# Six ring buffers instead of five for streamed weights, ten resident weights instead of eleven

## The chip, the cores and the metric

The kernel runs on one core of a Trainium2 chip. TensorE (matmuls), VectorE (DVE), ScalarE (ACT) and GpSimd (POOL) work side by side, each through its own list of instructions in order; SyncE (SP) issues nearly all DMA transfers of this kernel, also in order. An instruction may wait for semaphores of other engines or of transfers, and whatever stands behind it on its engine waits with it. The metric is the time of one execution on the device in microseconds, the median of several runs.

## The reference

One layer of graph attention with a layer norm ahead of it, over 128 graphs of 128 nodes and 768 features, in float32:

```python
h = jnp.maximum(_layernorm(x, axis=-1), 0.0)
x = x + _L0_gnn_ref(h, adj, Wq, bq, Wk, bk, Wv, bv, beta)

# _L0_gnn_ref, with 12 heads of 64:
q = _split_heads(input_graph @ Wq + bq)        # k and v likewise
scores = jnp.einsum('bhqd,bhkd->bhqk', q, k) / jnp.sqrt(HD)
scores = scores + beta * adj_e
scores = jnp.where(adj_e > 0, scores, -9000000000000000.0)
probs = jax.nn.softmax(scores, axis=-1)
out = jnp.einsum('bhqk,bhkd->bhqd', probs, v)
```

## The kernel before

**Tiling.** Four graphs make a group: 512 rows of activations, and 32 groups in all (`G` from 0 to 31). Each group needs the product of its normalised, transposed activations with Wq, Wk and Wv. The weights are taken in three slices: `qk0` (the first half of the columns of q and k), `v`, and `qk1` (the second half of q and k).

**Products.** In groups 1 to 31 a slice is a 2x3 by 3x3 block product done with 15 block multiplications instead of 18 (the table `PRODUCTS`), and each of these with seven 128x128 zones instead of eight. A group is thus 3 x 15 = 45 products; this text calls their places in the order slots 0 to 44: 0 to 14 are qk0, 15 to 29 are v, 30 to 44 are qk1. "v.5" means row 5 of `PRODUCTS` in the slice v. Each product reads one combination of activations, which DVE has summed before, and one *prepared weight*: seven 128x128 float32 tiles, 448 KB. `product` (line 664) issues 28 matmuls at line 681.

**Prepared weights.** During group 0, which works with plain products (`plain_slice`, line 1029), DVE and POOL build all 45 prepared weights from the raw ones (`prepare`, line 367; sums at lines 380 to 386 and 403). Those whose place in `sequence` is named in `RESIDENT` stay in SBUF for good (tiles `res_qk`, `res_v`, line 360). The others are built in a buffer, stored to DRAM once (`kept`, line 389) and loaded anew in each of the groups 1 to 31. `home` (line 369) picks the buffer: while qk0 and v are prepared, three of eight non-resident weights are built in a buffer with tag "e" (which later hold the attention's exponentials), all others in the ring.

**The ring.** Streamed weights land in the `RING` buffers with tag "T". `ring` (line 431) lists them in the order of use. `load_T` (line 435) issues the next load on SP. It is called as many times as there are buffers during group 0 (twice within `prepare`, and for `n in range(2, RING)` at line 1319), and then once behind each streamed product, at line 685. SP's instruction waits until that product's matmuls have read their buffer; the weight that it fetches is the one used `RING` streamed products later. A product with a resident weight calls no load.

**Order.** From the slice v of group 0 on all instructions stand in an order written out by hand (`manual_schedule`, line 1284): `slice_z` (line 1009) emits product by product, and behind each one what the tables `TABLE`, `EVICT` and `DECODE` give for that time. The products' results leave PSUM through DVE (lines 704, 711) and ACT (lines 716, 724, 726), are decoded on POOL (lines 739 to 754), and go to scores (line 776), masking (line 789), the exponential (line 798) and attention (line 855). SP's list holds the loads of weights, the loads of x in two forms (lines 295 and 513), of adj (line 599), of the residual (`xo`, line 763) and the outputs (line 908).

Of the kernel before, what the change touches and what calls it, by code (L numbers as in the profile page):

```python
# [114 lines left out]
PORDER = (1, 0, 5, 2, 3, 10, 7, 6, 13, 11, 4, 9, 14, 8, 12)  # L115
XORDER = (1, 0, 5, 2, 3, 10, 6, 7, 13, 11, 4, 9, 14, 8, 12)
ORDER = {"qk0": (1, 0, 5, 2, 10, 3, 6, 7, 13, 11, 9, 4, 14, 12, 8), "v": (1, 0, 5, 2, 10, 3, 6, 7, 13, 11, 4, 9, 14, 8, 12), "qk1": (4, 1, 0, 8, 2, 5, 3, 6, 7, 10, 9, 13, 11, 12, 14)}
RING = 5
RESIDENT = (10, 12, 16, 17, 21, 29, 33, 36, 39, 41, 42)
EB = 3  # L120
HOMES = 8

# [104 lines left out]
def direct(ctx, tc, x, adj, wq, bq, wk, bk, wv, bv, beta, out, bad):  # L227
# [131 lines left out]
    sequence = [(sl, n) for sl in ("qk0", "v", "qk1") for n in ORDER[sl]]  # L359
    resident = {key: const.tile([P, 7, P], F32, name=f"res_{key[0]}_{key[1]}") for key in (sequence[at] for at in RESIDENT)}  # L360
    kept, tz = {}, {}
# [5 lines left out]
    def prepare(sl):  # L367

        def home(name):
# [4 lines left out]
            if sl != "qk1" and made_in[0] % 8 in (2, 5, 7):  # L374
                t = work.tile([P, 2, W], F32, tag="e", name=f"prep_{sl}_{n}", bufs=EB)
                return t.rearrange("p i w -> p (i w)")[:, 0:7 * P].rearrange("p (z n) -> p z n", n=P)
            return work.tile([P, 7, P], F32, tag="T", name=f"prep_{sl}_{n}", bufs=RING)

# [56 lines left out]
    def load_T():  # L435
        if nt[0] < len(ring):
            G, sl, n = ring[nt[0]]
            nt[0] += 1
            t = tz[G, sl, n] = work.tile([P, 7, P], F32, tag="T", name=f"T_{G}_{sl}_{n}", bufs=RING)
            nc.sync.dma_start(t, kept[sl, n])  # L440
# [751 lines left out]
    def then(at, f, *args):  # L1192
        todo.setdefault(at, []).append(lambda: f(*args))
# [6 lines left out]
    def bias(G, *at):  # L1200
        for n in at:
            then(n, bias_step, G)
# [115 lines left out]
    bias(1, 4, 6, 8)  # L1318
    for n in range(2, RING):
        then(10 + n, load_T)  # L1320
# [180 lines left out]
```

## Time and profile before

| | us |
|---|---|
| median of 3 runs | 2683.88 |
| lowest, highest | 2681.6, 2685.84 |
| the profiled execution's own time | 2675.62 |
| its span in the profile | 2673.7 |
| granted TensorE clock over the span | 0.998 of full |

The profile is of one execution. PE stands for the matmuls of TensorE and PEld for its weight loads, which overlap; SPq for SP as it issues DMAs. A group of instructions is written as line, engine, operation and tiles, out<-in, so `pair<-sbig,T_qk` at L681 are the matmuls of a product of qk0 or qk1 with a streamed weight, `res_qk` and `res_v` mark resident ones, and `T_v` streamed ones of the slice v. "Idle before <- X" says what ended an engine's idle time; "issue" means that the profile shows nothing that did. The ends of matmuls are modelled, so matmul rows of neighbouring products overlap a little, and starts are the better measure. In rows by stretch (us from the span's start) come the stretch's length, the busy time of PE, PEld, DVE, ACT and POOL with their number of instructions, the granted clock, the mean busy share of the 16 DMA engines and the GB/s that they moved; a share can come out a little over 1. In the chain of waits each row is a piece of the work that ended last: start, length, what.

### The profile page before, as it was taken

Reading aid. Unit: us, or ns where it says so; the run is one execution under the profiler, and the core shown is the slowest. Engines: PE = TensorE matmul, PEld = TensorE weight load, DVE = VectorE, ACT = ScalarE, POOL = GpSimd, SP = SyncE. Lnnn points to the kernel's source line nnn. Section 1 sums busy time; section 2 is a strip of 40 time slices with the busy share of each in tenths; the row PEclk is TensorE's granted clock in tenths of the full one; section 3 lists DMA queues with packets and bytes.
Section 4 is the critical chain, followed back from the end, with each engine's and each line's share of the span. In section 5 each row is a group of like instructions: output and inputs, shape, how many; then the busy total and the mean of one; then the engine's idle time right before and its main releaser. Section 6 shows DMA issues by size and latency. Waiting matters only on the chain.

```text
span 2673.7 us, 121363 instructions
## 1 busy us (share of the span) xinstructions
PE 2645.9 (99%) x52041; PEld 2565.2 (96%) x52041; DVE 2165.9 (81%) x2702; ACT 1754.7 (66%) x4608; POOL 2089.9 (78%) x3043
## 2 busy tenths in 40 slices
PE   9999999999999999999999999999999999999998
PEld 8799999999999999999999999999999999999997
DVE  7878887878887778888788877888887888778876
ACT  2567766677766677666777666776667776667654
POOL 4877778877778877788777788777887777887774
PEclk9999999999999999999999999999999999999999
DMA  8888888888888988888888888889888888888875
GB/s 247 270 272 270 276 280 272 275 287 262 285 279 272 282 269 271 281 278 269 280 265 283 278 272 267 274 271 285 272 272 280 265 282 280 265 277 275 249 247 165
DMA packets 526964, 721.97 MB, mean 270 GB/s; under 512 B 105932, under 2 KB 370648, under 8 KB 526424
## 3 DMA queue, kind: packets, MB, share of 16 engines
q1 hardware_dynamic: 525776, 713.38, 84.4%
q8 instruction: 411, 6.73, 1.0%
q14 instruction: 129, 1.06, 0.1%
q10 hardware_dynamic: 648, 0.79, 0.1%
HBM read 647.99 MB, written 66.05 MB: 267 GB/s over the span
## 4 chain that ended last, share of the span: by engine, by line
PE 95%; DMA 3%; DVE 1%; issue 0%; SPq 0%; ACT 0%; ACTq 0%; DVEq 0%
PE pair L681 78%; PE pair L776 7%; PE pair L855 6%; PE pair L1048 3%; DMA T_qk<-kept_qk 2%; DMA sbig<-in_L_gnn_Wk_dram 0%; PE pair L1265 0%; DVE home L704 0%; PE pair L1053 0%; DMA x<-in_x_dram 0%; SPq L336 0%; PE pair L926 0%; SPq L908 0%; DVE e L789 0%; DVE st L464 0%
## 5 line engine op out<-in xcount | busy, mean ns | idle before, releaser
L704 DVE TENSOR_TENSOR home<-home,pair 128x896 f32<-128x896 f32 x836 | 880.8, 1077 | 225.5 <-PE pair L681 192.7
L681 PE MATMUL pair<-sbig,T_qk 128*64 128x128 f32 x13020 | 833.0, 274 | 9.2 <-DMA T_qk<-kept_qk 6.9
L681 PEld LDWEIGHTS pair<-sbig,T_qk 128*64 128x64 f32 x13020 | 711.6, 137 | 28.7 <-issue 16.5
L739 POOL TENSOR_TENSOR home<-home 128x256 f32<-128x256 f32 x308 | 263.5, 855 | 339.3 <-DVE home L704 339.0
L681 PE MATMUL pair<-A,T_qk 128*64 128x128 f32 x6944 | 446.0, 273 | 0.3 <-issue 0.3
L855 PE MATMUL pair<-v,e 128*64 128x65 f32 x6048 | 412.6, 221 | 0.7 <-issue 0.7
L681 PE MATMUL pair<-T_v,sbig 128*64 128x128 f32 x6944 | 404.1, 273 | 2.1 <-issue 1.5
L681 PEld LDWEIGHTS pair<-T_v,sbig 128*64 128x64 f32 x6944 | 382.2, 137 | 8.3 <-ACT e L836 5.0
L836 ACT ACTIVATE e<-e,sm 128x64 f32<-128x64 f32 x1512 | 381.7, 341 | 5.0 <-DVE sm L824 3.4
L681 PEld LDWEIGHTS pair<-A,T_qk 128*64 128x64 f32 x6944 | 384.0, 137 | 0.4 <-issue 0.4
L855 PEld LDWEIGHTS pair<-v,e 128*64 128x64 f32 x6048 | 370.7, 137 | 3.8 <-issue 0.8
L724 ACT ACTIVATE home<-pair 128x640 f32<-128x640 f32 x340 | 240.4, 707 | 189.0 <-PE pair L681 187.7
L681 PE MATMUL pair<-sbig,res_qk 128*64 128x128 f32 x4340 | 314.0, 273 | 0.3
L742 POOL TENSOR_TENSOR home<-home 128x256 f32<-128x256 f32 x308 | 264.3, 858 | 24.1
L885 ACT ACTIVATE sm<-pair,tiny 128x8 f32<-128x8 f32 x189 | 50.8, 269 | 338.4 <-PE pair L855 338.4
L789 DVE SCALAR_TENSOR_TENSOR e<-pair,biasT 128x1024 f32<-128x1024 f32 x189 | 229.3, 1213 | 34.1 <-PE pair L776 33.1
L740 POOL TENSOR_TENSOR home<-home 128x256 f32<-128x256 f32 x308 | 230.6, 749 | 24.1
L681 PEld LDWEIGHTS pair<-sbig,res_qk 128*64 128x64 f32 x4340 | 240.5, 137 | 1.4 <-DVE home L704 1.3
L560 ACT ACTIVATE x<-x,block 128x192 f32<-128x192 f32 x480 | 222.6, 540 | 0.0
L726 ACT ACTIVATE home<-pair,bqk 128x128 f32<-128x128 f32 x680 | 214.1, 377 | 0.0
L798 ACT ACTIVATE e<-e 128x1024 f32<-128x1024 f32 x189 | 196.1, 1055 | 20.3 <-DVE e L789 12.7
L741 POOL TENSOR_TENSOR home<-home 128x128 f32<-128x128 f32 x308 | 180.4, 586 | 24.2
(208 smaller groups left out, 4489.9 us busy)
## 6 DMA issues: line engine op xcount, KB each, us to landing
T_qk<-kept_qk SPq DMA_DIRECT2D x713, 448.0 KB, 4.7
T_v<-kept_v SPq DMA_DIRECT2D x341, 448.0 KB, 4.7
xo<-in_x_dram SPq DMA_DIRECT2D x190, 256.0 KB, 5.3
out_dram<-xo SPq DMA_DIRECT2D x189, 256.0 KB, 5.2
x<-in_x_dram SPq DMA_DIRECT2D x248, 192.0 KB, 7.6
sbig<-in_x_dram SPq DMA_DIRECT2D x116, 384.0 KB
kept_qk<-prep_qk SPq DMA_DIRECT2D x23, 448.0 KB, 2.8
adj<-in_adj_dram SPq DMA_DIRECT2D x128, 64.0 KB, 4.1
```

The costliest lines, as they stand in the source:

```text
L560: nc.scalar.activation(t, t, AF.Relu, bias=shift[G, n], scale=rstd[G, n])
L681: nc.tensor.matmul(p[q:q + HD, at, :], lhs[:, q:q + HD], rhs, start=(first and at % 4 == 0), stop=True, skip_group_check=True)
L704: nc.vector.tensor_tensor(t, t, p[:, 0:7], op)
L724: nc.scalar.activation(t[:, 0:5], p[:, 0:5], AF.Copy, scale=float(sign))
L726: nc.scalar.activation(t[:, at], p[:, at], AF.Identity, bias=bqk[:, of, oc:oc + 1], scale=float(sign))
L739: e.tensor_tensor(t[:, 1:4:2], t[:, 1:4:2], twice(5), ALU.add)
L740: e.tensor_tensor(t[:, 2:5:2], t[:, 2:5:2], twice(1), ALU.add)
L742: e.tensor_tensor(t[:, 0:7:6], t[:, 0:7:6], twice(2), ALU.add)
L789: nc.vector.scalar_tensor_tensor(e[:, :, at], ps[:, :, at], SCORE_CAP * ISCALE, bias[:, :, at], op0=ALU.min, op1=ALU.add)
L798: nc.scalar.activation(e, e, AF.Exp, scale=1.0 / ISCALE)
L836: nc.scalar.activation(o[:, r, b, 0:HD], pa[:, r, b, 0:HD], AF.Copy, scale=t[:, 1, r, b:b + 1])
L855: nc.tensor.matmul(pa[q:q + HD, 2 * g + i, :], k[:, q:q + HD], vt[G, "v", r, h // 4][:, 4 * g + h % 4, :], start=True, stop=True, skip_gro ...
```

## The change

`RING` goes from 5 to 6, and place 17 leaves `RESIDENT`. Place 17 of `sequence` is the third product of the slice v, v.5: its prepared weight (the sum T6 of `SUMS_B`) is built in a buffer, stored once, and streamed in each of the 31 groups. A resident tile and a ring buffer have the same size, so SBUF use stays. The order of the products and all tables stay. The count of streamed weights in a group goes from 34 to 35.

```diff
--- before.py
+++ after.py
@@ -115,8 +115,8 @@
 PORDER = (1, 0, 5, 2, 3, 10, 7, 6, 13, 11, 4, 9, 14, 8, 12)
 XORDER = (1, 0, 5, 2, 3, 10, 6, 7, 13, 11, 4, 9, 14, 8, 12)
 ORDER = {"qk0": (1, 0, 5, 2, 10, 3, 6, 7, 13, 11, 9, 4, 14, 12, 8), "v": (1, 0, 5, 2, 10, 3, 6, 7, 13, 11, 4, 9, 14, 8, 12), "qk1": (4, 1, 0, 8, 2, 5, 3, 6, 7, 10, 9, 13, 11, 12, 14)}
-RING = 5
-RESIDENT = (10, 12, 16, 17, 21, 29, 33, 36, 39, 41, 42)
+RING = 6
+RESIDENT = (10, 12, 16, 21, 29, 33, 36, 39, 41, 42)
 EB = 3
 HOMES = 8
```

## The prediction, made before the result was known

> **What bounds the kernel now.** I read the page first, for the engine that sets the end.
>
> ```profile
> span 2673.7 us, 121363 instructions
> ...
> PE 2645.9 (99%) x52041; PEld 2565.2 (96%) x52041; DVE 2165.9 (81%) x2702; ACT 1754.7 (66%) x4608; POOL 2089.9 (78%) x3043
> ...
> PE 95%; DMA 3%; DVE 1%; issue 0%; SPq 0%; ACT 0%; ACTq 0%; DVEq 0%
> ```
>
> TensorE is busy 99% of the span, and the chain of waits is 95% TensorE: the matmul stream is the bound. The change removes no matmul. It can win only the time in which that stream stands still for a streamed weight, and the 3% of the chain that runs through DMA says where to look. Next is the chain of waits in order of time, a few starts from the whole run.
>
> ```profile
> 161.29 9.32 PE pair L681 x168
> ...
> 568.51 9.32 PE pair L681 x168
> ...
> 649.53 9.32 PE pair L681 x168
> ...
> 2525.49 9.32 PE pair L681 x168
> ```
>
> This run of 168 matmuls in 9.32 us stands at the same slot of each group. Two neighbours are 649.53 - 568.51 = 81.02 us apart: an undisturbed group. From 161.29 to 2525.49 there are 2364.2 us; 29 undisturbed groups make 29 x 81.02 = 2349.6. So all irregular waits of 29 groups together cost 14.6 us, a ceiling for the gain there. One such wait, in three views: the chain, the matmuls, and SP's DMA issues.
>
> ```profile
> 2543.48 6.02 DMA T_qk<-kept_qk
> ```
>
> ```profile
> 2543.47 1.70 PE L681 MATMUL pair<-res_v,A 128*64 128x128 f32 x28
> 2545.00 1.70 PE L681 MATMUL pair<-A,T_qk 128*64 128x128 f32 x28
> 2546.53 1.70 PE L681 MATMUL pair<-sbig,T_qk 128*64 128x128 f32 x28
> 2549.64 1.60 PE L681 MATMUL pair<-sbig,T_qk 128*64 128x128 f32 x25 [1.41 <-DMA T_qk<-kept_qk]
> ```
>
> ```profile
> 2540.36 1.63 SPq L440 DMA_DIRECT2D T_qk<-kept_qk  x1
> 2542.09 1.29 SPq L908 DMA_DIRECT2D out_dram<-xo  x1
> 2543.48 0.46 SPq L440 DMA_DIRECT2D T_qk<-kept_qk  x1
> ```
>
> An undelayed product takes 1.53 us (2545.00 - 2543.47 with a resident weight, 2546.53 - 2545.00 with a streamed one), so a streamed weight that is there in time costs TensorE nothing. The fourth product, slot 32 of its group (qk1.0), had its load issued at 2543.48; it took 6.02 us and came 1.41 us late. The load before it, for slot 31, went out at 2540.36. SP, which issues in order, lost the time between on that issue (1.63 us) and on an output (1.29).
>
> **How large the stall is.** The waits of TensorE on loads; the idles in front of weight loads that read T_qk, by what ended them; the same view of a group without a stall:
>
> ```profile
> PE pair L681 <- DMA T_qk<-kept_qk: 6.9, 9, 1.4
> ```
>
> ```profile
>   issue: 16.9, 73
>   DVE adj L613: 2.1, 2
> ...
>   DVE A L580: 1.4, 1
>   DVE biasT L617: 1.0, 1
>   DVE biasT L605: 0.7, 1
> ```
>
> ```profile
> PEld pair L681 <- issue: 0.5, 3, 0.2
> ```
>
> Lower bound: 6.9 us in 9 waits that the matmul side lays to the load. Upper bound, from the weight side: in qk the streamed weight is what is loaded into the array, so the wait stands there first, and the profile names "issue" or some DVE instruction for it. 16.9 + 2.1 + 1.4 + 1.0 + 0.7 = 22.1 us. A quiet group has three idles of 0.17 us at L681 (0.5 in all), two of them in front of T_qk, so 31 x 2 x 0.17 = 10.5 us are regular and 22.1 - 10.5 = 11.6 remain. I take 10.5, near the upper end, since the wait begins on the weight side and short ones show only there.
>
> **The change part by part.** *A sixth buffer.* SP issues at the same places of the program as before, but each issue fetches the weight that is used one streamed product later. So a load goes out, and lands, about when its predecessor did. In the stall above, slot 32's load takes the place at 2540.36 and is 2543.48 - 2540.36 = 3.1 us earlier, against 1.41 us of lateness: it is there in time. Where SP isn't behind, the shift is one product, 1.53 us, still over the longest wait of 1.4. It holds for slots 24 (v.11) to 44 and on through qk0. Gain 10.5 us, if transfers take as long as before.
>
> *v.5 streamed.* Product 5 of the slice v (slot 17) reads a resident weight now; it gets one load in each of 31 groups. Up to v.13 (slot 23) the sixth buffer is used up by v.5 itself, so the leads of v.2, v.10, v.3, v.7 and v.13 stay. What the new load meets: TensorE's weight loads, SP's issues, and the DMA share by stretch, all in one group, with the row of the loads and of all DMA from the page.
>
> ```profile
> DMA packets 526964, 721.97 MB, mean 270 GB/s; under 512 B 105932, under 2 KB 370648, under 8 KB 526424
> ```
>
> ```profile
> T_v<-kept_v SPq DMA_DIRECT2D x341, 448.0 KB, 4.7
> ```
>
> ```profile
> 1376.93 3.09 PEld L681 LDWEIGHTS pair<-res_v,sbig 128*64 128x64 f32 x56
> ```
>
> ```profile
> 1377.30 13.03 SPq L440 DMA_DIRECT2D T_v<-kept_v  x5
> ```
>
> ```profile
> 1380.10:1383.70 3.60, 3.60 (x98) 3.33 (x96) 1.65 (x2) 3.48 (x11) 3.32 (x5) 1.00 0.89 274
> 1383.70:1387.30 3.60, 3.60 (x72) 3.60 (x70) 3.27 (x5) 3.54 (x9) 3.33 (x6) 1.00 0.63 222
> 1387.30:1392.50 5.20, 5.20 (x112) 4.86 (x108) 3.97 (x6) 3.71 (x8) 4.15 (x8) 1.00 0.70 228
> 1406.00:1412.00 6.00, 6.00 (x128) 6.00 (x126) 4.66 (x6) 2.45 (x8) 5.69 (x9) 1.00 1.05 412
> ```
>
> 31 x 448 KB are 14.2 MB, 2.0% over the 721.97 MB of now. The 56 weight loads of res_v are the two resident products v.0 and v.5, which end near 1380.1. The new load goes out there. SP waits there for TensorE, and behind the new wait stand only other weight loads: from 1377.30 to 1390.33 SP issues nothing but L440, so no load of x, no output and no row is held up. From 1380.1 to 1392.5 the DMA engines have room: 0.11 x 3.6 + 0.37 x 3.6 + 0.30 x 5.2 = 3.3 us of all sixteen. One load is 458,752 bytes: 1.1 us at the 412 GB/s of the last row, 1.7 us at the mean of 270. That room hides it: 0 us. Without the room the loads behind it would land 1.1 to 1.7 us later, and where the shift is one product the gain would be gone.
>
> The Trainium skill's "DMA: Bandwidth & Descriptors", section Specifications, puts the limit of HBM for one core at about 358 GB/s. The trace does not agree: the stretch from 1406 moved 412 GB/s. By the page's figure the added bytes would be an estimated 14.2 MB / 358 GB/s = 40 us where nothing hides them; by the rows they fit into the idle share.
>
> *At the start.* The weight of v.5 is made by the same instructions and now also stored, once; which later weights of v are made in the ring and which in the buffers of e changes with it. The nearest rows:
>
> ```profile
> SPq L389 <- POOL prep_v L386: 14.0, 7, 3.7
> ```
>
> ```profile
> DVE prep_qk L403 <- POOL prep_v L386: 2.5, 1, 2.5
> ```
>
> SP waits for a weight to be ready for its store, 2.0 us on the mean, 3.7 at most; DVE waits 2.5 us once. One store more holds SP for up to 3.7 us, under plain products that keep TensorE going; a sixth buffer can save DVE its 2.5. Bounds on the path: -2.5 to +3.7 us. I take 0, since DVE at 81% and SP have time to spare and TensorE is the bound.
>
> *At the end* nothing is left to load: 0. Sum against the profiled execution: 2675.6 us (its span of 2673.7 and 1.9 around it) - 10.5 = 2665.1. That execution lies 8.3 us under the median of the timed runs, 2683.88; I carry the difference over: 2683.9 - 10.5 = 2673.4, or 0.39% faster. What is late next are the 0.17 us idles and a few single ones, which stay.
>
> **The rivals.** *Late loads stay late.* At the start of qk1 the DMA share is 1.05, so transfers queue; if the added load is not worked off by then, each landing there moves out by 1.1 to 1.7 us. For it: that share. Against it: the room of 3.3 us before, and a shift of 3.1 us where SP was behind. Gain 0 to 7, middle 3: 2681.
>
> *More was lost in the timed runs.* The 8.3 us between profile and median may be late loads too. For it: the stalls differ from group to group (none in the quiet one, 1.4 us in another), so they depend on more than the program. Against it: a constant part is as likely. Gain 10.5 + 8.3 = 18.8: 2665.
>
> *Instruction fetch*, the slower side. TensorE has idles that no semaphore ends:
>
> ```profile
> 2200.85 2.21 PEld L681 LDWEIGHTS pair<-T_v,sbig 128*64 128x64 f32 x40 [0.89 <-issue]
> ```
>
> ```profile
> q8 instruction: 411, 6.73, 1.0%
> ```
>
> This one lies in the first products behind the scores of v, where the new load will be in flight. I read it as a late fetch: 411 packets in 2673.7 us are one in 6.5 us, so each group has one near this place. If a fetch there waits until the new load has passed (middle 1.4 us) in all 31 groups, it costs 31 x 1.4 = 43 us; less 10.5 the time is 2683.9 + 33 = 2717. It decides from 8 groups on (8 x 1.4 = 11.2). For it: the place. Against it: loads are in flight nearly always already, and the ceiling for all irregular waits is 14.6 us.
> The Trainium skill's "DMA: Bandwidth & Descriptors", section Queues, rings and completion order, says that each DMA engine takes turns between queues packet by packet; by that rule a fetch waits for a packet and not for the load, the cost is near 0 and the time the forecast's. No run here shows the turns.
>
> **How the numbers follow.** Forecast 0.63, late loads 0.15, more to win 0.10, fetch 0.07, and 0.05 for a build that differs elsewhere, on the slow side. About 0.2% (5.4 us) is what a measurement of this kernel can tell from no change. Faster by more than that: forecast and second rival, 0.73. The same: most of the first rival, 0.14. Slower: fetch, the differing build and the rest, 0.13. The forecast's own range: 10.5 becomes 6.9 to 11.6 and the start -2.5 to +3.7, so 2670 to 2681. The whole range takes in the second rival's 2665 and the first rival's end at no gain, with 3.7 us at the start, each with some of the runs' scatter of 2 us: 2662 to 2688. Outside lies mostly the fetch.
>
> **What would show it.** Right: no wait of TensorE on T_qk above 0.3 us, groups 81.0 us apart nearly throughout, 341 + 31 = 372 loads of T_v, and 1% or less of DMA in the chain. Late loads: landings at the start of qk1 over 6 us and idles that remain there. Fetch: idles put down to "issue" behind the scores of v in most groups. The prediction is wrong if TensorE stops for DVE or ACT where it stopped for the load, with the same time per group, or if the groups stay as far apart as now.

## The result and the profile after

| | before | after |
|---|---|---|
| median, us (executions) | 2684.86 (4) | 2666.82 (4) |
| lowest to highest, us | 2681.6 to 2686.05 | 2664.59 to 2668.08 |
| the profiled execution's own time, us | 2675.62 | 2665.87 |
| its span, us | 2673.7 | 2664.1 |

The ratio of the times is 0.9934, with a 95% interval of 0.9917 to 0.9951: the change saves 18.0 us, or 0.66%. 2673.4 had been forecast, inside a range of 2662 to 2688 that holds the measured time. Measured between the two profiled executions the gain is only 9.75 us, near the 10.5 of the sum; the experiments had to explain the difference of the two gains as well as the gain.

From the page of the kernel after, the span, the engines, all DMA, the chain by engine, and the issues of T_v:

```profile
span 2664.1 us, 121442 instructions
PE 2644.1 (99%) x52041; PEld 2564.2 (96%) x52041; DVE 2165.8 (81%) x2702; ACT 1755.1 (66%) x4608; POOL 2097.8 (79%) x3043
...
DMA packets 531572, 736.65 MB, mean 277 GB/s; under 512 B 106444, under 2 KB 371160, under 8 KB 531032
...
PE 94%; DVE 1%; DMA 0%; issue 0%; ACT 0%; SPq 0%; DVEq 0%; ACTq 0%
...
T_v<-kept_v SPq DMA_DIRECT2D x372, 448.0 KB
```

TensorE still has its 52,041 matmuls and is still the bound. The 3% of DMA in the chain are gone, although the kernel moves 736.65 - 721.97 = 14.7 MB more and issues the 341 + 31 = 372 loads of T_v that were announced.

The waits of TensorE's matmuls in the kernel after, in the view that gives for each the line, what it waited for, the total, how often and the longest; these are its first rows and a later one, at the start of the kernel:

```profile
PE pair L1369 <- DVE over L970: 3.6, 1, 3.6
PE pair L681 <- issue: 2.4, 6, 1.1
PE pair L681 <- DVE home L704: 2.2, 2, 1.2
...
PE pair L1048 <- ACT home L1065: 1.2, 1, 1.2
```

and the idles in front of TensorE's weight loads that read T_qk, by what ended them, all rows:

```profile
  issue: 13.6, 67
  DVE home L704: 1.6, 2
  DVE sbig L585: 0.2, 1
```

No wait on a load of T_qk is left on the matmul side, where there were 6.9 us in 9 waits. On the weight side 22.1 us have become 13.6, of which 10.5 are the regular 0.17 us idles, so 8.5 us are gone there. The 3.1 us that stay over the regular ones belong to five further idles that no semaphore ends. At L681 no wait of the matmuls on another engine grew.

The groups, by one piece of the chain of waits that comes once in each (start, length, what):

```profile
171.94 15.65 PE pair L681 x284
...
2446.97 15.65 PE pair L681 x284
2527.99 15.65 PE pair L681 x284
```

The last two are 81.02 us apart, the undisturbed group of before. From first to last there are 29 groups in 2356.05 us, so 2356.05 - 29 x 81.02 = 6.5 us are irregular, where 14.6 were. That is 8.1 us of the 9.6 by which the span is shorter; the other 1.5 lie before the first or behind the last of these rows.

The place of the stall, in group 30. SP's issues of the kernel after:

```profile
2529.71 0.32 SPq L440 DMA_DIRECT2D T_qk<-kept_qk  x1
2530.08 2.52 SPq L599 DMA_DIRECT2D adj<-in_adj_dram  x4
2532.70 0.70 SPq L440 DMA_DIRECT2D T_qk<-kept_qk  x1
2533.50 1.27 SPq L908 DMA_DIRECT2D out_dram<-xo  x1
2534.86 0.68 SPq L440 DMA_DIRECT2D T_qk<-kept_qk  x1
```

and its matmuls of slots 31 and 32:

```profile
2538.67 3.23 PE L681 MATMUL pair<-sbig,T_qk 128*64 128x128 f32 x56
```

SP is as far behind as before: the four issues of adj take it 2.52 us and the output 1.27. But the load between them, at 2532.70, is slot 32's now and no longer slot 31's. Of the 56 matmuls from 2538.67 the second half, slot 32, begins at 2538.67 + 1.53 = 2540.20, 7.5 us behind its load. In the stall of before its load had 2546.53 + 1.53 - 2543.48 = 4.6 us, and took 6.02.

The added load of v.5, in the same stretches of the same group of the kernel after, 3.0 us earlier on its clock:

```profile
1377.10:1380.70 3.60, 3.60 (x96) 3.33 (x94) 1.65 (x2) 3.48 (x11) 3.32 (x5) 1.00 1.08 333
1380.70:1384.30 3.60, 3.60 (x71) 3.60 (x69) 3.14 (x5) 3.54 (x9) 3.34 (x6) 1.00 0.75 228
1384.30:1389.50 5.20, 5.20 (x111) 4.95 (x107) 3.88 (x5) 3.57 (x8) 4.02 (x8) 1.00 0.77 244
```

The next to last column, the share of the DMA engines, was 0.89, 0.63 and 0.70. The rise makes 0.19 x 3.6 + 0.12 x 3.6 + 0.07 x 5.2 = 1.5 us of all sixteen: the load, between the 1.1 and 1.7 estimated. TensorE, in the column behind the length, is busy throughout.

The start of group 1, one wait for DVE that every run has (start, length, what, the idle in front). First before, then after:

```profile
134.50 1.75 PE L681 MATMUL pair<-sbig,T_qk 128*64 128x128 f32 x28 [1.19 <-DVE home L704]
```

```profile
134.77 1.75 PE L681 MATMUL pair<-sbig,T_qk 128*64 128x128 f32 x28 [1.19 <-DVE home L704]
```

The kernel after comes here 0.27 us later.

### The profile page after: what moved, and what is told of

Its sections match the earlier page's. It is cut to its first block, busy times and chain, and to the rows that moved or that the text cites. A ratio compares the mean times of both kernels' runs of the same rounds, so it can differ in the third digit from the quotient of the medians.

```text
span 2664.1 us, 121442 instructions
## 1 busy us (share of the span) xinstructions
PE 2644.1 (99%) x52041; PEld 2564.2 (96%) x52041; DVE 2165.8 (81%) x2702; ACT 1755.1 (66%) x4608; POOL 2097.8 (79%) x3043
## 2 busy tenths in 40 slices
DMA packets 531572, 736.65 MB, mean 277 GB/s; under 512 B 106444, under 2 KB 371160, under 8 KB 531032
## 4 chain that ended last, share of the span: by engine, by line
PE 94%; DVE 1%; DMA 0%; issue 0%; ACT 0%; SPq 0%; DVEq 0%; ACTq 0%
PE pair L681 80%; PE pair L776 7%; PE pair L855 6%; PE pair L1048 1%; DVE home L704 0%; DMA x<-in_x_dram 0%; DMA T_qk<-kept_qk 0%; PE pair L926 0%; DVE e L789 0%; DVE prep_qk L403 0%; ACT e L836 0%; DVE res_qk L403 0%; PE pair L947 0%; DVE e L931 0%; ACT e L933 0%
## 5 line engine op out<-in xcount | busy, mean ns | idle before, releaser
L681 PE MATMUL pair<-sbig,T_qk 128*64 128x128 f32 x13020 | 827.6, 274 | 2.3 <-DVE home L704 1.2
L681 PEld LDWEIGHTS pair<-sbig,T_qk 128*64 128x64 f32 x13020 | 702.5, 137 | 19.9 <-issue 12.1
L681 PE MATMUL pair<-T_v,sbig 128*64 128x128 f32 x7812 | 457.8, 273 | 1.6 <-ACT home L716 0.6
L681 PE MATMUL pair<-A,T_qk 128*64 128x128 f32 x6944 | 445.6, 273 | 0.9 <-issue 0.9
L681 PEld LDWEIGHTS pair<-T_v,sbig 128*64 128x64 f32 x7812 | 430.7, 137 | 8.4 <-ACT e L836 4.8
L855 PE MATMUL pair<-v,e 128*64 128x65 f32 x6048 | 403.5, 221 | 0.0
L681 PEld LDWEIGHTS pair<-A,T_qk 128*64 128x64 f32 x6944 | 384.6, 137 | 1.5 <-issue 1.5
L855 PEld LDWEIGHTS pair<-v,e 128*64 128x64 f32 x6048 | 362.2, 137 | 3.2
L681 PE MATMUL pair<-sbig,res_qk 128*64 128x128 f32 x4340 | 312.3, 273 | 0.4
L681 PEld LDWEIGHTS pair<-sbig,res_qk 128*64 128x64 f32 x4340 | 238.0, 137 | 1.4 <-DVE home L704 1.3
```

The costliest lines, as they stand in the source:

```text
L681: nc.tensor.matmul(p[q:q + HD, at, :], lhs[:, q:q + HD], rhs, start=(first and at % 4 == 0), stop=True, skip_group_check=True)
L855: nc.tensor.matmul(pa[q:q + HD, 2 * g + i, :], k[:, q:q + HD], vt[G, "v", r, h // 4][:, 4 * g + h % 4, :], start=True, stop=True, skip_gro ...
```

## The experiments

The theory: SP, held up by the four issues of adj (and an output), sends the loads of slots 31, 32 and 34 late; one more buffer sends each out one streamed product earlier; and it is the spread of these late loads over executions that made 18.0 us of 10.5. The rivals: the difference of 8.3 us between the profiled execution and the median is constant and something else gave the rest; the loads are late for want of DMA bandwidth; the taking of v.5 out of SBUF, not the buffer, is what counts.

The last column measures the stall where it stands. In the profiled execution of each run it adds up, over the groups 2 to 30, the time from the first matmul of slot 30 to the first of slot 36. An undisturbed group takes 10.10 us for it; in the kernel after every group does, which makes 293.0 us, and in the kernel before the sum is 303.7.

Ratios are against runs of the kernel before made beside each experiment (medians 2685.03 for e1 to e4, 2685.89 for e5 to e8, 2687.45 for e9 to e12).

| run | buffers | what differs | median us (lowest to highest, executions) | ratio (95%) | slots 30 to 35, us |
|---|---|---|---|---|---|
| e1_before_again | 5 | nothing | 2683.35 (2677.06 to 2691.82, 10) | 0.9995 (0.9981 to 1.0008) | 312.1 |
| e2_ring5_res10 | 5 | v.5 streamed | 2685.74 (2678.28 to 2698.65, 10) | 1.0011 (0.9997 to 1.0025) | 303.4 |
| e3_adj_early | 5 | adj issued earlier | 2667.93 (2665.83 to 2672.15, 4) | 0.9937 (0.9920 to 0.9954) | 293.1 |
| e4_swap_32 | 5 | qk1.0 resident, v.5 not | 2670.15 (2669.16 to 2673.03, 4) | 0.9951 (0.9934 to 0.9967) | 297.3 |
| e5_adj_on_act | 5 | adj issued by ACT | 2667.79 (2666.07 to 2671.07, 4) | 0.9935 (0.9918 to 0.9951) | 294.7 |
| e6_six_and_adj | 6 | after, and adj earlier | 2664.67 (2664.18 to 2666.59, 4) | 0.9921 (0.9905 to 0.9938) | 293.1 |
| e8_six_drop_33 | 6 | place 33 gives the buffer | 2672.41 (2669.10 to 2673.99, 4) | 0.9944 (0.9927 to 0.9961) | 301.7 |
| e7_ring7_res9 | 7 | places 16, 17 give buffers | 2661.87 (2661.22 to 2666.49, 4) | 0.9908 (0.9891 to 0.9924) | 293.0 |
| e9_after_again | 6 | the kernel after | 2668.51 (2667.18 to 2671.72, 6) | 0.9936 (0.9920 to 0.9952) | 293.0 |
| e10_ring7_again | 7 | as e7 | 2663.11 (2661.47 to 2667.06, 6) | 0.9917 (0.9901 to 0.9934) | 293.1 |
| e11_ring7_act | 7 | e7, adj by ACT | 2662.94 (2662.38 to 2667.70, 6) | 0.9917 (0.9901 to 0.9934) | 293.7 |
| e12_swap_act | 5 | e4, adj by ACT | 2671.89 (2666.22 to 2675.65, 6) | 0.9949 (0.9931 to 0.9967) | 293.3 |

### Is the difference between profile and median late loads too?

e1 is the kernel before, unchanged, to have the profile of another of its executions.

> The kernel before, unchanged, profiled a second time. Its first profiled execution took 2675.62 us, its other runs 2681.6 to 2686.05. Theory (the rest of the gain is more late loads): an execution near 2684 us shows 15 to 20 us of waits of TensorE on loads of T_qk on the matmul side, not the 6.9 of the first profile, again at the first products of qk1. Rival (a constant part of some 8 us outside): the waits on T_qk stay at 6 to 8 us and the longer time is found elsewhere. Ratio to before: 1.00.

Its profiled execution took 2683.59 us, 8.0 more than the one before the prediction. First its largest wait on the matmul side, then its chain:

```profile
PE pair L681 <- DMA T_qk<-kept_qk: 11.7, 14, 2.8
```

```profile
161.85 9.32 PE pair L681 x168
...
2533.99 9.33 PE pair L681 x168
```

From 161.85 to 2533.99 there are 2372.14 us, 22.6 more than 29 x 81.02, against 14.6 in the other execution: 8.0 us, all of the difference, lie in irregular waits. The wait on loads rose from 6.9 us in 9 to 11.7 in 14 on the matmul side, short of the 15 to 20 that had been expected there; on the weight side the idles in front of T_qk that no semaphore ends rose from 16.9 to 25.5, while those laid to adj, A and biasT, 5.2 us before, are gone. The sum over slots 30 to 35 needs no such names: 312.1 us against 303.7 before, 8.4 more. The longest wait, in the matmuls and in SP's issues:

```profile
2473.91 2.04 PE L681 MATMUL pair<-sbig,T_qk 128*64 128x128 f32 x28 [2.77 <-DMA T_qk<-kept_qk]
```

```profile
2460.85 2.02 SPq L599 DMA_DIRECT2D adj<-in_adj_dram  x4
2462.96 2.36 SPq L440 DMA_DIRECT2D T_qk<-kept_qk  x1
2465.43 0.97 SPq L908 DMA_DIRECT2D out_dram<-xo  x1
```

It is slot 32 again, and the same place in SP's list: adj, one slow load, an output. So the 8.3 us that the prediction carried over as a constant were late loads, of which the execution profiled first had few. Against the kernel after the same sum is 312.1 - 293.0 = 19.1 us, and the two executions differ by 2683.59 - 2665.87 = 17.7: these six slots hold the whole gain.

### Which half of the change does it?

```diff
 RING = 5
-RESIDENT = (10, 12, 16, 17, 21, 29, 33, 36, 39, 41, 42)
+RESIDENT = (10, 12, 16, 21, 29, 33, 36, 39, 41, 42)
```

> The added traffic alone: v.5 is streamed as in the changed kernel, but the ring keeps five buffers. Theory (the gain is the longer lead, and the added load is hidden by idle DMA time behind the scores of v): the leads of v.2 to v.13 shrink by one product and those behind are as before, so the stall at the start of qk1 stays as it was and the time is that of before within 5 us, 2680 to 2690. Rival (the added load pushes the later loads back): the waits on T_qk grow by 1.1 to 1.7 us in most of 31 groups, 2700 to 2730.

The traffic of the change without its buffer moves nothing: ratio 1.0011, and the stall is there, by the wait on the matmul side:

```profile
PE pair L681 <- DMA T_qk<-kept_qk: 5.7, 10, 1.1
```

So the 31 added loads cost nothing that can be told from noise (0.25% at the upper end of the interval), and the gain is the buffer's. The buffer without the traffic was not tried: it would need the place of one tile more than the kernel before.

In e8 the sixth buffer is paid for by another resident, place 33, the one that comes right behind the late slots:

```diff
-RING = 5
-RESIDENT = (10, 12, 16, 17, 21, 29, 33, 36, 39, 41, 42)
+RING = 6
+RESIDENT = (10, 12, 16, 17, 21, 29, 36, 39, 41, 42)
```

> Six buffers as in the changed kernel, but the resident that pays for the sixth is qk1.8 (slot 33), right in the stretch where the loads queue, and v.5 stays resident. Theory that the place of the added load matters: slots 34 and 35 keep the lead they had before, one load more stands in the full stretch, slots 31 and 32 gain a product; some waits remain at slot 34, the time is 2668 to 2680. Rival that only the number of buffers matters: 2664 to 2668 as the changed kernel.

The waits of e8 on the matmul side, and one of them at its place:

```profile
PE pair L681 <- DMA T_qk<-kept_qk: 5.3, 10, 1.3
```

```profile
2058.21 1.70 PE L681 MATMUL pair<-A,T_qk 128*64 128x128 f32 x28
2061.22 0.44 PE L681 MATMUL pair<-sbig,T_qk 128*64 128x128 f32 x4 [1.31 <-DMA T_qk<-kept_qk]
```

The late load is slot 34's now, behind a slot 33 that reads T_qk too (the row at 2058.21): with one more load on the bad stretch, the sixth buffer is used up there. The kernel is still faster than before, by 0.56%. Its profiled execution, the longest of its four, loses 8.7 us in slots 30 to 35, where after loses none. By the medians it is 5.6 us slower than after, but the two were not timed beside each other, and their ratios, 0.9944 and 0.9934, differ by 2.7 us with intervals that overlap. Six buffers alone don't end the waits; the load has to be added where leads are long.

### Is it SP's list, or the bandwidth?

e3 leaves five buffers and eleven residents and moves the issues of adj ahead by 6.7 places in the order (the table counts slots, not us), from slot 24 to slot 17, where SP's loads have time:

```diff
-    (-23.578, 'inner', 'A01'), (-20.844, 'adj'), (-18.417, 'inner', 'A02'), (-20.599, 'turn', 'A11'),
+    (-23.578, 'inner', 'A01'), (-27.5, 'adj'), (-18.417, 'inner', 'A02'), (-20.599, 'turn', 'A11'),
```

> The kernel before with five buffers and eleven residents; only the four transfers of adj are issued at slot 17 instead of slot 24. Theory that SP's order makes the loads late (SP spends 2.3 us on the four transfers of adj just before the loads for qk1.1 and qk1.0): the loads go out up to 2.3 us earlier, most of the stall at the start of qk1 goes without a sixth buffer, and the time falls by 6 to 16 us to 2669 to 2679. Rival that the DMA engines are full at that place and only more lead helps: the landing of these loads moves by less than 0.5 us and the time stays within 4 us of before.

e5 leaves adj at its place in the order and has ACT issue it, so that the same bytes should be in flight at about the same time:

```diff
-            nc.sync.dma_start(t[a * SQ:(a + 1) * SQ].rearrange("p g b j -> p (g b) j"), src[a])
+            (nc.scalar if G > 1 else nc.sync).dma_start(t[a * SQ:(a + 1) * SQ].rearrange("p g b j -> p (g b) j"), src[a])
```

> The kernel before with five buffers and eleven residents; the four transfers of adj are issued at slot 24 as before, but by ACT and not by SP, from group 2 on. The bytes move at the same time, only SP is free of some 2.3 us. Theory that the loads were late because SP had other transfers to issue: the loads for qk1.1 and qk1.0 go out up to 2.3 us earlier, the waits of TensorE on T_qk fall below 2 us and the time is 2664 to 2672. Rival that adj's small packets fill the DMA engines just ahead of these loads: they are issued earlier but land no earlier, the stall stays over 5 us and the time over 2678.

Both are as fast as the kernel after, 0.9937 and 0.9935 against 0.9934; e3 gained a little more than the 16 us expected at most. SP's list around slot 30 of the same group, in e3 and then in e5:

```profile
2519.15 3.68 SPq L599 DMA_DIRECT2D adj<-in_adj_dram  x4
...
2535.84 1.85 SPq L440 DMA_DIRECT2D T_qk<-kept_qk  x2
2537.78 0.39 SPq L908 DMA_DIRECT2D out_dram<-xo  x1
2538.90 0.32 SPq L440 DMA_DIRECT2D T_qk<-kept_qk  x1
```

```profile
2529.89 1.85 SPq L440 DMA_DIRECT2D T_qk<-kept_qk  x2
2531.82 0.39 SPq L908 DMA_DIRECT2D out_dram<-xo  x1
2532.94 0.32 SPq L440 DMA_DIRECT2D T_qk<-kept_qk  x1
```

and in the kernel before, ahead of and in the stall that the prediction shows:

```profile
2537.57 0.32 SPq L440 DMA_DIRECT2D T_qk<-kept_qk  x1
2537.94 2.33 SPq L599 DMA_DIRECT2D adj<-in_adj_dram  x4
2540.36 1.63 SPq L440 DMA_DIRECT2D T_qk<-kept_qk  x1
...
2543.48 0.46 SPq L440 DMA_DIRECT2D T_qk<-kept_qk  x1
```

Without adj between them the first two loads go out within 1.85 us, the output takes 0.39 us where it took 1.29, and the third load goes out 3.06 us behind the first in e3 and 3.05 in e5, the time of two products of 1.53 us: SP keeps pace with TensorE. Before, the third load went out 2543.48 - 2537.57 = 5.9 us behind the first, and 5.2 in the kernel after (2534.86 - 2529.71). Neither in e3 nor in e5 do the matmuls wait for a load of T_qk, and of the 10.7 us that slots 30 to 35 lost before, e3 still loses 0.1 and e5 1.7. In e3 the issues of adj stand 16.7 us ahead of the first load, where they stood 0.4 behind it: they moved by 17 us, and so did adj's bytes. So e3 alone can't tell SP's list from the bandwidth.

e5 comes nearer, but adj does not go out quite as before in it. ACT's issues of adj:

```profile
2527.64 0.86 ACTq L599 DMA_DIRECT2D adj<-in_adj_dram  x2
...
2528.54 1.92 ACTq L599 DMA_DIRECT2D adj<-in_adj_dram  x2
```

They start 2.25 us ahead of the first load, at 2529.89, and no longer 0.37 behind it, since they don't stand behind SP's wait for slot 24: 2.6 us earlier, in each group. What speaks against the bandwidth is how long the loads took. In e5 the load for slot 31 took 5.7 us to land, the median of groups 2 to 30, and 7.3 at most, much like the 6.02 us of the late load for slot 32 before. It was in time because it went out 7.4 us ahead of its slot's first matmul in every group. Before, that lead was 6.1 us at the median for slot 31 and 5.5 for slot 32, and transfers as long as those of e5 would often have come late there too. So the leads that SP's list takes away explain the stall; that adj's bytes, 2.6 us earlier, eased it a little as well is not ruled out.

The Trainium skill's "DMA: Bandwidth & Descriptors", section Issuing engines are not separate DMA queues, says that DMAs started on several engines share the same 16 DMA engines, and that this saves only the time of the issue, usually small beside the DMA. The trace agrees for one transfer: an issue of adj takes SP 0.49 us at the median, beside 4.1 us until it has landed. But four in a row, 2.33 us in the group shown, stand between two loads of a stream that uses one every 1.53 us, and having ACT issue them was worth 18.1 us of the whole (2685.89 - 2667.79).

e4 takes the late slot out instead, by making slot 32's weight resident:

```diff
-RESIDENT = (10, 12, 16, 17, 21, 29, 33, 36, 39, 41, 42)
+RESIDENT = (10, 12, 16, 21, 29, 32, 33, 36, 39, 41, 42)
```

> Five buffers and eleven residents, but qk1.0 (slot 32, where most of the stall is) is resident in place of v.5 (slot 17). The traffic is that of before. Theory (the stall is lateness of single loads at slots 31 to 34): slot 32 cannot stall, the loads for slots 34 and 35 go out one product earlier, only slot 31 with 1 to 3 us in all remains, and the time is 2667 to 2673, as with six buffers. Rival (the DMA engines cannot deliver at that rate, whoever is resident): the stall moves to slots 30, 31 or 34 and the time stays above 2679.

Most of the gain is there (0.9951), and slots 30 to 35 lose 4.3 us. What is left of that stands in the idles of the matmuls that read T_qk:

```profile
  DMA T_qk<-kept_qk: 2.1, 1
  DVE adj L613: 1.4, 1
```

Both are at slot 31, whose load also goes out behind adj. The profile lays the second to DVE; I read it as a late load too, since a product's matmuls do not read adj, but no run shows that by itself.

### Do the gains add?

> The changed kernel (six buffers, ten residents) with the transfers of adj issued at slot 17. Theory that both remove one and the same stall: the gains do not add, the time is that of the changed kernel within 4 us, 2663 to 2671. Rival that each removes a stall of its own: 18 + 17 us below before, near 2650.

e6 is the kernel after with e3's edit. It takes 2664.67, 2.2 us less than the kernel after (timed apart from it, with intervals that overlap), while each edit alone saves 17 to 18. They remove one and the same stall.

e7 goes one step on: seven buffers, with v.2 (place 16) streamed as well.

```diff
-RING = 5
-RESIDENT = (10, 12, 16, 17, 21, 29, 33, 36, 39, 41, 42)
+RING = 7
+RESIDENT = (10, 12, 21, 29, 33, 36, 39, 41, 42)
```

> One step further: seven buffers and nine residents (v.0 streamed too, 31 more loads). Theory that six buffers already end every wait on a load: no further gain, 2663 to 2671, with the DMA share one or two hundredths higher. Rival that the traffic begins to count (idles before the matmuls behind the scores of v, or loads late again): slower than the changed kernel by over 5 us, above 2672.

It came out at 2661.87, 5.0 us under the kernel after. That was not expected, since with six buffers no wait on T_qk is left to remove, and so both were run again side by side, as e9 and e10.

> The changed kernel once more, beside the next three on the same chip: 2664 to 2668 us, no wait of TensorE on T_qk, idles without a semaphore at slots 9, 18 and 19 as in its first profile, 1 to 4 us in all.

> Seven buffers and nine residents again, with more rounds: its four runs lay some 4 us under those of the changed kernel. Theory (no wait on a load is left in either, so nothing can be won): it is equal to the changed kernel within 2 us. Rival (timed runs of the changed kernel still hold a few late loads): 3 to 5 us faster again.

2668.51, a little above the range expected, and 2663.11: 5.4 us again, though the two intervals (0.9920 to 0.9952, 0.9901 to 0.9934) overlap a little. It is not late loads at the start of qk1: slots 30 to 35 take 293.0 and 293.1 us. Part of it lies at the start. The wait of group 1 shown above comes at 133.17 in e7 and at 132.80 in e10, against 134.77 in after and 136.40 in e9, that is 1.6 to 3.6 us earlier. This is e10's row:

```profile
132.80 1.75 PE L681 MATMUL pair<-sbig,T_qk 128*64 128x128 f32 x28 [1.19 <-DVE home L704]
```

But after and e9, one and the same kernel, lie 1.6 us apart there too. From group 2 to group 31 e10 is 2.5 us shorter than e9, but e7 2.3 longer than after; these are single executions. Whether seven buffers start earlier, and why, was not settled.

> Seven buffers, nine residents, and adj's transfers issued by ACT. Both remedies of the late loads at once: if late loads were all, 2660 to 2666 as with seven buffers alone; if anything is left in SP's order, 3 us or more under it.

> Five buffers, qk1.0 resident in place of v.5, adj issued by ACT: no sixth buffer and the traffic of before. Theory (the stall is only late loads at slots 31, 32 and 34): 2661 to 2667, as good as six or seven buffers with 2 to 4% less traffic. Rival (fewer bytes leave fewer idles without a semaphore): under 2660.

e11 is e7 with adj issued by ACT; it adds nothing to e7. e12 is e4 with adj issued by ACT and was to be as fast as the kernel after; it took 2671.89, with six executions from 2666.22 to 2675.65. Its profiled execution, 2667.06 us, is one of the short ones. It shows no late load, only a longer wait at the start than the 1.2 us of the kernel after:

```profile
PE pair L1048 <- ACT home L1065: 3.2, 1, 3.2
```

What the longer executions of e12 have was not seen, and why its median is 5.1 us above that of the kernel after stays open. The best version measured is e7's, with seven buffers and nine residents: both times it was the fastest of those run beside it or within 0.2 us of that.

## Why the prediction was right, and where its size was off

**What bounds it.** Right. TensorE did the same 52,041 matmuls, undisturbed groups are 81.02 us apart as before, and the whole gain is time in which they stood still for streamed weights.

**How large the stall is.** This is the term that was mis-sized, in being carried over from one execution to the median. The step took 10.5 us from 6.9 to 11.6, both read from one execution. For that execution it was right: slots 30 to 35 held 303.7 - 293.0 = 10.7 us (8.5 went from the weight side and 8.1 from the chain, which also count other idles). For the timed runs it was much too low: the step that carries 8.3 us over to the median as a constant failed. e1 shows an execution near the median, with 8.0 us more of irregular waits, and 8.4 us more in these six slots. So the stall is about 18 us in the median, and the rival that more was lost in the timed runs (18.8 us, 2665, given a chance of 0.10) is the case that came true, by the forecast's own mechanism. That the measured time lies inside the range is owed to that rival, not to the forecast's own range of 2670 to 2681.

**The sixth buffer.** Right. The place in SP's list that fetched slot 31's weight now fetches slot 32's, SP is late as before, and the shift outweighs it: 7.5 us of lead where 4.6 were too few. e2 shows that streaming v.5 alone does not do it, e3 and e5 that without adj between the loads the stall is gone at five buffers. The prediction gave SP's lag to the slow issue and the output, and did not name the four issues of adj ahead of them, without which both take their usual 0.32 and 0.39 us in the groups shown.

**v.5 streamed.** Right at nothing, by the DMA share (1.5 us of an estimated 3.3 of room) and by e2. e8 suggests that this nothing belongs to the place: with one load more behind adj's issues, 8.7 us of late loads are left, though by the times its loss against the kernel after, 2.7 to 5.6 us, is not clear of noise.

**Start and end.** Bounds of -2.5 to +3.7, taken as 0: the trace has +0.27 us at the wait of group 1, but e9, the same kernel again, comes there 1.6 us behind after. The bounds were fair and the zero is not better known than that.

**The rivals.** *Late loads stay late* is false here, since no such wait is left. With another resident given up such waits do stay (e8), but the gain there is still 13.5 us by the medians, beyond the 0 to 7 that this rival gave. *Instruction fetch* did not happen. The idles of all weight loads at L681 that no semaphore ends, first before and then after:

```profile
PEld pair L681 <- issue: 24.6, 108, 1.6
```

```profile
PEld pair L681 <- issue: 20.5, 103, 1.3
```

They became fewer, where 31 more of 1.4 us had been feared.

*A differing build*: the loads came out as counted. The signs announced as right are all there: no wait laid to a load of T_qk, 81.0 us between groups, 372 loads, 0% of DMA in the chain.

## What to carry to other kernels

A stall for a late transfer can differ much between executions of one kernel: here it was 10.7 us in one and 19.1 in another. One profile gave its place well and its size badly; where the profiled execution lies far from the median, ask first whether the same stall explains it, before the difference is carried over as a constant. When loads are late, look at what stands between them in the list of the engine that issues them: here a buffer, a move of four small issues, or another engine for them were worth the same 17 to 18 us, and only one of them costs SBUF. And a deeper ring leaves part of the waits if what pays for it puts a load into the stretch that it is to relieve.

## What the runs showed of the hardware that was not expected

With loads that are barely in time the whole time scatters: executions of the kernel before, with the repeated e1, lie between 2675.62 and 2696.24 us, those of the kernel after between 2664.59 and 2671.72.

The issue of a DMA can take long. The row of SP's issues of T_qk gives the shortest, the median and the longest in ns; here it is for the kernel before:

```profile
L440 SPq DMA_DIRECT2D T_qk<-kept_qk x713: 319/320/3638, 101.0 to 2640.1; - x179
```

In the rows shown the slow ones stand directly behind the four issues of adj (1.63 us before, 2.36 in e1, 0.70 after), and the output behind them is slow too (1.29, 0.97 and 1.27 us against 0.39 in e3 and e5). So those four seem to cost SP more than their own 2.0 to 2.5 us; what makes the issues behind them slow, no run shows.

And TensorE has idles that nothing in the profile ends, in every kernel profiled. The longest at L681 in e9, in the weight loads, with the stretches before and in it:

```profile
1464.60 3.52 PEld L681 LDWEIGHTS pair<-T_v,sbig 128*64 128x64 f32 x64 [2.01 <-issue]
```

```profile
1459.00:1461.00 2.00, 2.00 (x55) 1.83 (x55) 0.67 (x2) 1.72 (x6) 1.84 (x4) 1.00 1.10 401
...
1463.00:1465.00 2.00, 0.40 (x8) 0.40 (x9) 0.00 (x0) 1.94 (x5) 1.84 (x4) 1.00 0.34 125
```

It follows on a stretch in which the DMA engines were full (share 1.10) and lies in one in which they and DVE are mostly idle. Whether a late transfer of instructions is behind it stays open: no run here was made to show that.
